# A transformer stack on one core: attention values weighted by features instead of by tokens, with a new order of the steps

## Chip, core and metric

The kernel runs on one NeuronCore of one Trainium2 chip. The metric is the device time of one execution in microseconds, the median of several runs; less is better. All data are float32.

## The reference

The input is 8 sequences of 512 tokens with 128 features. First comes one attention layer with squared-kernel features (stage one, not touched by the change but for one detail). Then six layers follow, each with a local attention and a feed-forward part. Cut to what matters:

```python
for i in range(6):
    t = shift_tokens(x)                      # second half of the features one token later
    q, k, v = heads(t @ Wqkv[i])             # 16 heads of 64
    q, k = l2norm(q) * qs, l2norm(k) * ks
    q, k = rotary(q), rotary(k)              # with a scale by position
    # windows of 32 tokens; each sees its own window and the one before: 64 keys
    sim = einsum('bhwie,bhwje->bhwij', q_w, k_2w) * 8
    attn = softmax(where(mask, -big, sim), -1)
    out = einsum('bhwij,bhwje->bhwie', attn, v_2w)
    x = out @ Wo[i] + x
    h = layernorm(shift_tokens(x)) * g + b
    a, gate = split(h @ W1[i] + b1)
    x = (a * gelu(gate)) @ W2[i] + b2 + x
```

A residual and layer norms stand around both stages.

## The kernel before, in words

The residual stream of each sequence lies in SBUF with features on partitions (`state`, L54). Work of the six layers is cut into **units** of 128 tokens: 6 layers x 8 sequences x 4 blocks = 192 units, made at L681 to L685. Four successive units are one sequence; below they are called a batch.

The loop over t (L703 to L739) is a software pipeline written out by hand. Turn t, a **slot**, runs steps of several units: `at(t, lag, step)` (L688) runs `step` for unit t-lag; with `ends=True` only for the last unit of a sequence. TensorE's order is exactly the order of these calls (manual schedule, L694). The orders of the other engines are made by a scheduler that places each instruction by its own estimate, with `tc.high_priority()` moving some ahead, and `issue_behind(later, earlier)` (L86) fixing an order of two instructions on one engine. Every engine then runs its instructions in that fixed order.

The steps of a slot, in TensorE's order:

- `proj(t, 0)` and `proj(t, 1)` (L409): q and k, two 128x512 products each into the PSUM ring `mm` (two buffers of two banks, L419). VectorE multiplies by the rotary tables (`turned` twice L429, `straight` L436), ScalarE squares (L444), GpSimd adds (L454). `sum_squares` (L456) sums the squares on VectorE; the one for k is put behind the last division by `issue_behind` (L461).
- `out_project(t-3)` (L598): eight products with the output weights, added into `state` by VectorE (L608).
- `by_keys(t-2)` (L556): eight transposes of the exponentials `pe`, copied out by ScalarE into `pT` (L564).
- `values(t)` (L474): v, two products, one ScalarE copy of both halves (L482) and eight DMAs that spread v to windows (L489, L490, L492).
- `by_features(t-1, 0)` and `(t-1, 4)` (L498): eight transposes each of q and k, copied by ScalarE (L514).
- `weigh_values(t-2)` (L566): 64 small products, with the weights (`pT`, 64 keys x 32 tokens) loaded and v (64 keys x 64 features) streamed. The result `po` has tokens on partitions. VectorE divides by the row sums as it copies out (`on`, L582).
- `feed_norm`, `feed_first`, `feed_middle`, `feed_last` (L611, L637, L648, L653), once in four slots each: norm over features after transposing `state` (its four transposes L616 go to ring `mm`), back to features, hidden products with Gelu, last product.
- `unit_length(t)` (L463): inverse root of the sums on ScalarE (`inverse_root`, L93), a minimum and two products on GpSimd (L467, L470).
- `scores(t-1)` (L519): the mask is put in by two products with the identity (L527), then 64 small products (L534). VectorE takes the maxima (`mx`, L542), ScalarE 16 exponentials (L546), VectorE the row sums `su` and their reciprocals (L552, L553).
- `out_by_features(t-2)` (L588): eight transposes of `on`, copied by ScalarE into `oT` (L596), which `out_project` of the next slot needs.

`sp` and `po` share one PSUM buffer of two banks (tag `s`, L525, L569), all transposes and `py` share a ring of two banks (tag `tr`). ScalarE needs two tables, one with logarithm and exponential (L76) and one with Gelu (L82); each batch loads both once.

## Time and profile before

| what | us |
|---|---|
| median of 3 runs (lowest, highest) | 3898.34 (3889.66, 3900.85) |
| the profiled execution itself | 3893.85 |
| its span by the profile | 3892.1 |
| TensorE busy, of 3892.1 | 3729.8 |
| VectorE / ScalarE / GpSimd busy | 2818.2 / 2657.5 / 1837.0 |
| L582, division, 192 times | 235.1 |
| L596, copies of `oT`, 384 times | 207.3 |
| L574, weighted values, 24576 records | 299.3 |
| L534, scores, 24576 records | 312.2 |
| transposes of `on`, 1536 records | 216.5 |
| L527, mask products, 384 records | 114.6 |

The granted TensorE clock is 0.99 of full speed. In the lines of groups, a row gives source line, engine, operation, the tile written and those read, the shapes, the count; then busy time, mean ns of one, and idle time of the engine before them with what ended it. In the chain and the timeline a row starts with the start and the duration in us. A float32 product is two records on TensorE, a transpose one; a small share of the records can be missing. The means of single matmuls contain their latency (225 ns for L574), so their cost is read from the chain's pieces, not from the means.

### The profile page before, as it was taken

What the parts mean: (1) busy time and instruction counts of PE and PEld (TensorE: products, weight loads), DVE (VectorE), ACT (ScalarE), POOL (GpSimd) and SP (SyncE); (2) the same over time, 40 slices, a digit from 0 to 9 for tenths busy, and PEclk for the clock granted to TensorE, in tenths of its full rate; (3) what the DMA queues carried; (4) which work ended last, traced back from release to release, by engine and by line L of the source; (5) the groups of instructions that cost most, each with busy time, mean ns of one, the idle gap of its engine ahead of it and who ended that gap; (6) DMA issues with size and microseconds to landing.
All of it is one profiled execution on the core that took longest, in us unless ns stands there. A gap on an engine that the chain in (4) does not pass through costs nothing.

```text
span 3892.1 us, 149565 instructions
## 1 busy us (share of the span) xinstructions
PE 3729.8 (96%) x65600; PEld 2474.2 (64%) x65600; DVE 2818.2 (72%) x4300; ACT 2657.5 (68%) x6745; POOL 1837.0 (47%) x1311
## 2 busy tenths in 40 slices
PE   8999989999999999999999999999999999999997
PEld 4555456666666666666666666666666666666665
DVE  4555567777867777777777777777787777777775
ACT  5565656776767777777777677777677777766664
POOL 0000025555555555555555555555555555555552
PEclk9999999999999999999999999999999999999998
DMA  2000012222222222222222322223222222222221
GB/s 81 17 9 12 6 50 71 59 66 60 76 74 63 63 63 66 71 75 65 60 62 64 82 65 66 65 56 82 70 66 59 66 65 56 65 68 68 64 67 37
DMA packets 153208, 233.46 MB, mean 60 GB/s; under 512 B 32622, under 2 KB 53356, under 8 KB 151788
## 3 DMA queue, kind: packets, MB, share of 16 engines
q1 hardware_dynamic: 152556, 223.89, 22.4%
q8 instruction: 517, 8.47, 0.9%
q14 instruction: 135, 1.11, 0.1%
HBM read 24.54 MB, written 4.19 MB: 7 GB/s over the span
## 4 chain that ended last, share of the span: by engine, by line
PE 89%; ACT 5%; issue 3%; DVE 2%; DMA 0%; POOL 0%; POOLq 0%; DVEq 0%; SPq 0%; ACTq 0%
PE tr L70 17%; PE mm L421 17%; PE mm L481 9%; PE py L603 9%; PE sp L534 7%; PE po L574 6%; PE y L282 4%; PE mm L625 3%; PE py L657 3%; PE mm L626 3%; PE sc L252 2%; PE sp L527 2%; ACT sq L444 2%; PE vv L230 2%; PE po L318 2%
## 5 line engine op out<-in xcount | busy, mean ns | idle before, releaser
L454 POOL TENSOR_TENSOR qk<-t,t 128x1024 f32<-128x1024 f32 x384 | 909.2, 2368 | 999.6 <-DVE t L436 999.5
L421 PE MATMUL mm<-wqkv,state 128*128 128x512 f32 x1536 | 727.1, 596 | 3.7 <-ACT v L482 2.6
L470 POOL TENSOR_TENSOR qk<-qk,ss 128x1024 f32<-128x1024 f32 x384 | 722.3, 1902 | 16.0
L429 DVE TENSOR_TENSOR t<-mm,tab 128x512 f32<-128x512 f32 x768 | 497.8, 685 | 242.8 <-PE mm L421 231.3
L546 ACT ACTIVATE pe<-sp,mx 128x64 f32<-128x64 f32 x3072 | 651.4, 376 | 27.6 <-DVE mx L542 27.3
L436 DVE TENSOR_TENSOR t<-mm,tab 128x1024 f32<-128x1024 f32 x384 | 465.9, 1213 | 0.0
L457 DVE TENSOR_REDUCE ss<-sq 128x16 f32<-128x1024 f32 x384 | 461.9, 1203 | 2.0 <-ACT sq L444 2.0
L444 ACT ACTIVATE sq<-mm 128x512 f32<-128x512 f32 x768 | 422.6, 610 | 47.2 <-DVE t L436 45.6
L603 PEld LDWEIGHTS py<-oT,wo 128*128 128x128 f32 x3072 | 374.8, 193 | 93.5 <-issue 56.2
L70 PEld LDWEIGHTS tr<-ident,qk 128*128 128x128 f32 x3072 | 345.7, 141 | 127.1 <-issue 105.7
L70 PE MATMUL tr<-ident,qk 128*128 128x128 f32 x3072 | 412.1, 277 | 7.4 <-ACT qT L514 2.3
L596 ACT COPY oT<-tr 128x512 f32<-128x512 f32 x384 | 207.3, 589 | 266.2 <-PE tr L70 265.2
L421 PEld LDWEIGHTS mm<-wqkv,state 128*128 128x128 f32 x1536 | 264.1, 192 | 191.6 <-issue 188.0
L481 PE MATMUL mm<-wqkv,state 128*128 128x512 f32 x768 | 367.9, 602 | 16.8 <-ACT sq L444 16.8
L603 PE MATMUL py<-oT,wo 128*128 128x128 f32 x3072 | 376.0, 276 | 1.0 <-ACT oT L596 0.9
L582 DVE TENSOR_TENSOR on<-po,su 128x1024 f32<-128x1024 f32 x192 | 235.1, 1224 | 170.1 <-PE po L574 170.1
L534 PEld LDWEIGHTS sp<-kT,qT 64*32 64x32 f32 x24576 | 271.9, 106 | 116.7 <-issue 113.8
L574 PE MATMUL po<-v,pT 64*32 64x64 f32 x24576 | 299.3, 225 | 44.7 <-issue 44.7
L482 ACT COPY v<-mm 128x1024 f32<-128x1024 f32 x192 | 194.5, 1013 | 211.0 <-PE mm L481 211.0
L534 PE MATMUL sp<-kT,qT 64*32 64x64 f32 x24576 | 312.2, 227 | 26.0 <-issue 25.2
L574 PEld LDWEIGHTS po<-v,pT 64*32 64x32 f32 x24576 | 258.5, 105 | 86.4 <-issue 86.2
L542 DVE TENSOR_REDUCE mx<-sp 128x16 f32<-128x1024 f32 x192 | 234.6, 1222 | 106.9 <-PE sp L534 106.3
(108 smaller groups left out, 5171.0 us busy)
## 6 DMA issues: line engine op xcount, KB each, us to landing
v<-v SPq DMA_DIRECT2D x1152, 128.0 KB
v<-v SPq DMA_DIRECT2D x672, 64.0 KB
wqkv<-in_L_ffn_Wqkv_dram SPq DMA_DIRECT2D x6, 1536.0 KB
wo<-in_L_ffn_Wo_dram SPq DMA_DIRECT2D x6, 512.0 KB
xin<-_attn_hidden_states_dram SPq DMA_DIRECT2D x8, 256.0 KB
xr<-_attn_hidden_states_dram SPq DMA_DIRECT2D x8, 256.0 KB
x<-xr SPq DMA_DIRECT2D x8, 256.0 KB
xr<-x SPq DMA_DIRECT2D x8, 256.0 KB
```

The lines of the kernel that those rows point to most:

```text
L70: nc.tensor.transpose(ps[:cols, :rows], src, ident[:rows, :rows])
L421: nc.tensor.matmul(ps[:, a].rearrange("p h d -> p (h d)"), lhs, wqkv[:, s, a, :], start=True, stop=True)
L429: nc.vector.tensor_tensor(t2[:, a], ps[:, 1 - a], tab[:, 2 * s + 1, j, HF * a : HF * (a + 1)].unsqueeze(1).to_broadcast([P, H, HF]), ALU.mult,
L436: nc.vector.tensor_tensor(t1, ps, tab[:, 2 * s, j, :].rearrange("p (a d) -> p a d", a=2).unsqueeze(2) .to_broadcast([P, 2, H, HF]), ALU.mult,)
L444: nc.scalar.activation(sq[:, :, a, :], ps[:, a], AF.Square)
L454: nc.gpsimd.tensor_tensor(qk[:, s].rearrange("p h a d -> p a h d"), t1, t2, ALU.add)
L470: nc.gpsimd.tensor_tensor(t, t, ss[:, i, :].unsqueeze(2).to_broadcast([P, H, HD]), ALU.mult)
L481: nc.tensor.matmul(ps[:, p, :], lhs, L["wqkv"][:, 2, p, :], start=True, stop=True)
L534: nc.tensor.matmul(sp[W * w : W * (w + 1), p, pair, :], qT[HD * p : HD * (p + 1), pair, W * w : W * (w + 1)], kT[HD * p : HD * (p + 1), pa ...
L546: ex = nc.scalar.activation(pe[:, pair, p, :], sp[:, p, pair, :], AF.Exp, bias=mx[:, p, pair : pair + 1])
L574: nc.tensor.matmul(po[W * w : W * (w + 1), p, pair, :], pT[r, pair, W * w : W * (w + 1)], v2[r, w, HD * pair : HD * (pair + 1)], start=Tru ...
L603: nc.tensor.matmul(py, L["wo"][:, c, :], oT[:, c, :], start=(c == 0), stop=(c == NP - 1))
```

## The change

1. `weigh_values` swaps its operands: v (64 keys x 64 features) is loaded and `pT` (64 keys x 32 tokens) is streamed, so `po` comes out with features on partitions. `on`, its division and `out_by_features` go; VectorE copies one half of `po` into `oT`, ScalarE the other. The rows of Wo are put in the matching order ahead of the launch.
2. The division moves before the transposes of `pe`: a new step `shares` (lag 2, ahead of `proj(t, 1)`) takes sums and reciprocals for each half of the heads on VectorE and divides `pe` in place on GpSimd.
3. `sp`, `po` and stage one's `y` become two tiles of one bank each (tags `s0`, `s1`), with maxima, exponentials and sums by half.
4. The mask products contract over 32 rows with a new constant `each`, apart from each sequence's first block.
5. `values` is cut into halves around `by_keys`; its copy and DMAs become `spread`, later in the slot. `by_features` is called for q and k apart, `squared` and `add_turned` become steps of their own.
6. `feed_norm` is split: `feed_in` transposes and copies (ScalarE) at lag 3, `feed_norm` follows at lag 4, `feed_first` moves to lag 5.
7. New `issue_behind` orders; the one that put the sum of k's squares behind the division goes. The Gelu table's load follows the copies of `pT`.
8. Once a batch, `addr_align(128, offset=46)` pads TensorE's instruction stream so that the next instruction stands 46 places after a multiple of 128.

```diff
     def gelu_only():
         ld = nc.scalar.preload_act_table_set("gelu_and_others")
-        issue_behind(ld, exps[-1])
+        issue_behind(ld, pcopies[-1])
...
+    def squared(u, s):
+        sq, ps = u["sq", s], u.pop(("psum", s))
+        for a in range(2):
+            q2 = nc.scalar.activation(sq[:, :, a, :], ps[:, a], AF.Square)
+            if s == 0 and exps:
+                issue_behind(q2, exps[-1])
+            if s == 1 and "cp" in u:
+                issue_behind(q2, u["cp"])
         if s == 0:
-            sum_squares(u, 0)
-        nc.gpsimd.tensor_tensor(qk[:, s].rearrange("p h a d -> p a h d"), t1, t2, ALU.add)
+            qsquares.append(q2)
+
+    def add_turned(u, s):
+        t1, t2 = u.pop("parts")
+        add = nc.gpsimd.tensor_tensor(u["qk"][:, s].rearrange("p h a d -> p a h d"), t1, t2, ALU.add)
+        if divisions:
+            issue_behind(add, divisions[-1])
...
-        if s == 1 and divisions:
-            issue_behind(su, divisions[-1])
+        if s == 0:
+            issue_behind(su, u["straight"])
...
+        nc.tensor.matmul(ps[:, half, :], lhs, L["wqkv"][:, 2, half, :], start=True, stop=True)
+
+    def spread(u):
+
+        j, v0 = u["j"], u["v0"]
+        cp = nc.scalar.copy(v0, u.pop("v0ps"))
+        if "cp" in u:
+            issue_behind(cp, u["cp"])
...
-        mk = mask0 if u["j"] == 0 else mask
-        sp = psum.tile([P, 2, NP, 2 * W], F32, tag="s", name="sp", bufs=1)
+        sp = [psum.tile([P, NP, 2 * W], F32, tag=f"s{p}", name="sp", bufs=1) for p in range(2)]
         for p in range(2):
+            r = slice(W * p, W * (p + 1))
+            lhs, mk = (identb, mask0) if u["j"] == 0 else (each[r], mask[r])
...
+    def shares(u):
+
+        pe = u["pe"]
+        for p in range(2):
+            part = pe[:, :, p]
+            su = f2.tile([P, NP], F32, tag=f"su{p}", name="su")
+            red = nc.vector.tensor_reduce(su, part, AX.X, ALU.add)
+            if sums:
+                issue_behind(red, sums[-1])
+            rc = nc.vector.reciprocal(su, su)
+            sums.append(rc)
+            with tc.high_priority():
+                dv = nc.gpsimd.tensor_tensor(
+                    part, part, su.unsqueeze(2).to_broadcast([P, NP, 2 * W]), ALU.mult
+                )
+        divisions.append(dv)
...
-        po = psum.tile([P, 2, NP, HD], F32, tag="s", name="po", bufs=1)
...
+        po = [psum.tile([P, NP // 2, P], F32, tag=f"s{p}", name="po", bufs=1) for p in range(2)]
+        for k in range(NP // 2):
             for w in range(4):
-                for p in range(2):
...
+                for i in range(2):
+                    for p in range(2):
+                        r, c, o = slice(HD * p, HD * (p + 1)), 2 * k + i, HD * (i ^ p)
+                        nc.tensor.matmul(
+                            po[p][o : o + HD, k, W * w : W * (w + 1)],
+                            v2[r, w, HD * c : HD * (c + 1)],
+                            pT[r, c, W * w : W * (w + 1)],
+                            start=True, stop=True, skip_group_check=True,
+                        )
+        u["oT"] = oT = f1.tile([P, 2, NP // 2, P], F32, tag="oT", name="oT")
         with tc.high_priority():
...
+            nc.vector.tensor_copy(oT[:, 0], po[0])
+            nc.scalar.copy(oT[:, 1], po[1])
...
         u["xn"] = xn = f1.tile([P, NB, DM], F32, tag="xn", name="xn")
-        layer_norm(f2, xn, ps, NB, by_log=True)
+        with tc.high_priority():
+            nc.scalar.copy(xn, ps)
+
+    def feed_norm(u):
+        layer_norm(f2, u["xn"], u["xn"], NB, by_log=True)
...
+            at(t, 0, proj, 0)
+            at(t, 3, out_project)
+            at(t, 0, squared, 0)
+            at(t, 2, shares)
+            at(t, 0, add_turned, 0)
+            at(t, 0, proj, 1)
+            at(t, 0, add_turned, 1)
+            at(t, 0, sum_squares, 0)
...
+            at(t, 1, by_features, 0, 0)
+            at(t, 1, by_features, 0, 1)
+            if t % NB == 0 and t <= len(units) - NB * (B - 1):
+                nc.tensor.addr_align(128, offset=IN_STEP)
+            at(t, 0, values, 0)
+            at(t, 2, by_keys)
+            at(t, 0, values, 1)
             if gelus:
                 gelu_only()
...
+            at(t, 5, feed_first, ends=True)
+            at(t, 1, by_features, 4, 0)
+            if 0 < t < len(units):
+                units[t]["cp"] = units[t - 1]["cp"]
+            at(t, 0, squared, 1)
             at(t, 2, weigh_values)
+            at(t, 4, feed_norm, ends=True)
             at(t, 0, sum_squares, 1)
             if not gelus:
                 at(t, 0, unit_length)
+            at(t, 1, by_features, 4, 1)
...
+            at(t, 3, feed_in, ends=True)
+            at(t, 0, spread)
             at(t, 5, feed_middle, ends=True)
...
             at(t, 6, feed_last, ends=True)
             at(t, 1, scores)
-            at(t, 2, out_by_features)
```

## The prediction

> **What bounds the kernel now.** I read the busy line and the chain first, then the chain in order of time over some slots, the timeline of the other engines, and the groups for durations. A slot is one turn of the loop over t (L703); four slots make a batch.

> ```profile
> PE 3729.8 (96%) x65600; PEld 2474.2 (64%) x65600; DVE 2818.2 (72%) x4300; ACT 2657.5 (68%) x6745; POOL 1837.0 (47%) x1311
> ...
> PE 89%; ACT 5%; issue 3%; DVE 2%; DMA 0%; POOL 0%; POOLq 0%; DVEq 0%; SPq 0%; ACTq 0%
> ```

> TensorE is the bound: 89% of the chain. One slot, from the end of the scores on:

> ```profile
> 1534.15 1.02 PE tr L70 x8
> 1535.17 1.72 PE mm L421 x4
> 1536.89 1.78 PE py L603 x16
> 1538.67 1.72 PE mm L421 x4
> 1540.39 0.87 PE tr L70 x8
> 1541.27 1.72 PE mm L481 x4
> 1542.98 0.88 PE tr L70 x8
> 1543.86 1.36 PE po L574 x88
> 1545.22 1.29 issue
> ```

> The reader is to see that PE goes from one step to the next without a gap: transposes of `on`, projection of q, output product, projection of k, transposes of `pe`, values, transposes of q and k, weighted values. The one hole is 1.29 us "issue" inside `po`. Scores start at 565.7 us and for the last time at about 3845.4 (timeline of L534), so 191 slots take 3280 us: 17.17 us a slot, **68.7 us a batch**.

> The other engines over the start of such a slot; the scores end, and the next step starts, at 1588.14:

> ```profile
> 1588.25 1.23 DVE L542 TENSOR_REDUCE mx<-sp 128x16 f32<-128x1024 f32 x1 [0.44 <-PE sp L534]
> ...
> 1591.06 1.29 DVE L429 TENSOR_TENSOR t<-mm,tab 128x512 f32<-128x512 f32 x2 [1.59 <-PE mm L421]
> 1592.27 1.21 DVE L436 TENSOR_TENSOR t<-mm,tab 128x1024 f32<-128x1024 f32 x1
> ...
> 1594.01 1.22 DVE L552 TENSOR_REDUCE su<-pe 128x16 f32<-128x1024 f32 x1
> ```

> The sum `su` is far down DVE's queue, 2.95 us after the first product with q's projection (1591.06), and nothing on PE waits for it soon: the transposes of `pe` need only the exponentials. Rows that price the change:

> ```profile
> L470 POOL TENSOR_TENSOR qk<-qk,ss 128x1024 f32<-128x1024 f32 x384 | 722.3, 1902 | 16.0
> ...
> L457 DVE TENSOR_REDUCE ss<-sq 128x16 f32<-128x1024 f32 x384 | 461.9, 1203 | 2.0 <-ACT sq L444 2.0
> ...
> L212 PE MATMUL vs<-cb,tw 128*128 128x4 f32 x128 | 15.6, 254 | 1.1 <-ACT tqk L222 1.0
> ```

> [...] L212 streams 4 columns and still takes 15.6/128 = 122 ns for 128 columns loaded [...] L574 and L534, 64x32 tiles, need 11 ns a record (1.41 us for 128); no row of before has a 64x64 tile. [...]

> **The change, part by part.**

> *Transposes of `on`* (8 a slot, 1.02 us of PE), the DVE product L582 (1.22) and two ACT copies L596 (0.54 each) go. In their place one DVE copy of half the size (0.69, as L234's 687 ns) and one ACT copy (0.59).

> *Weighted values by features.* 64 products as before, but 64 columns loaded and 32 streamed. [...] scaled by L212's 122 ns, 15. I take 128 x 14.6 = 1.87 us, an estimate, against 1.42. [...]

> *Masks.* In three slots of four they contract over 32 rows in two row groups; 0.43 becomes 0.22 to 0.43, I take 0.30.

> *Division moved to POOL, ahead of the transposes of `pe`.* Two products of 128x512 in the form of L470: half of 1.90, 0.95 to 1.05; I take 1.0. Bounds 0.5 and 1.3 (L327's 1266 ns for 512 plain columns). POOL has room (47%), but this puts DVE's sums and POOL on the path to PE. In the built order of the changed kernel DVE runs `mx` twice, the three products of q, two state additions, and then sum, reciprocal, sum, reciprocal. From the scores' end: products at 1.99 (PE's projection of q must end first; in the trace it began at 1589.07, after the 0.93 of the transposes that go, and the products at 1591.06), L436's at 3.20, state 4.33 (1593.40 in the same view, less the same 1589.07), first sum 4.94 to 5.63, reciprocal to 5.90, second sum 5.83 to 6.52, reciprocal to 6.79. POOL divides from 6.04 to 7.04 and to 8.04, and **the transposes of `pe` start at 8.2**. PE reaches them at 1.72+1.78+1.72+0.87+0.86 = 6.95: a new wait of 1.2 us a slot.

> *Order on ACT and DVE behind it.* Let b be that start. PE: transposes and second half of v to b+1.74, then four transposes of q. ACT copies them (b+2.38 to 2.97), and only then squares k (1.09, to b+4.03). DVE's sum of squares waits for this (b+4.13 to 5.34), and the copy out of `po` stands behind it on DVE (b+5.26 to 5.95), though `po` ended at b+4.06. The masks need that bank: b+6.0, where PE would be ready at b+4.5. Before, the copy out of `po` stood ahead of the sum. Scores end at b+6.0+0.3+1.45 = **b+7.75**. A plain slot is 8.2+7.75 = 15.95, whatever `po` takes up to 3.3 us.

> *Norm later.* By emission it moves a slot on; in the built order DVE still runs it in the slot of `feed_in`, wholly ahead of `mx`, and it now starts from an ACT copy. ACT: square to b+4.03, `oT`, k, `xn` copy to b+6.0; DVE: statistics 0.88 and 0.36 to b+7.25; ACT: v copy, then logarithm and exponential to b+7.96; DVE: four products to b+9.4. `mx` of the next slot starts 1.65 late, which is 0.9 at its products (2.9 for 1.99): b = 9.1 there.

> *Halves of v, spread.* Same 1.72 us of PE; v's copy is still in time for its bank and its DMAs keep more than a slot. Nothing on the path; if it slipped, projection of k would wait. *Alignment*: the batch is 2552 PE instructions, padded to 2560: 8 paddings at about 5.5 ns (256 in 1.41 us), nothing. The fetch holes (1.0 to 1.5 us, about two a batch) lie where PE now waits for the masks anyway: nothing left. *Five more table loads* at the stage edges: 5 x 1.28 = 6 us.

> Sum of a batch. Feed slot with the hidden products (5.2 us PE; the table load delays the square of k, and v's copy delays the second chunk): 20.65. Slot with the last product (2.58 hides the mask wait): 8.2+1.74+0.45+1.87+0.45+2.58+0.3+1.42 = 17.0. Slot with `feed_in`: 15.95. Slot after it: 9.1+7.75 = 16.85. **70.45 for 68.7**, so 191 slots cost 191 x (70.45-68.7)/4 = 84 us more, with the table loads 90: span 3982, execution 3984 (before: 3892.1 and 3893.85, which is 4.5 under the median shown, 3898.3). I predict **3980 us, slower by about 2%**. PE itself would need only some 62 us a batch: the change frees PE and is held by the ring mx, sums, division, transposes, square, sum, copy, masks, scores.

> **The rivals.**

> *Faster: the ring closes when PE arrives.* Place: POOL's division and the half sums. For it: every size there is scaled from whole tiles, and PE has 6 us a batch to gain. Against it: DVE's order is fixed and each link has a duration. If b is 7.0 where PE arrives, 191 x 1.2 = 230 us come off: 3750. It decides at b = 7.75 (0.45 less in each of four slots is the 1.75 of the sum): below it the kernel is faster. With a division of 0.5 us b is about 7.6: 3870.

> *Loads of 64 columns side by side fail*: `po` 3.7 us. It shows in full in the two feed slots (1.8 each) and by 0.35 in the others: 4.3 a batch, 205 us, 4185. For it: no 64x64 row; against it: the 64x32 tiles overlap more than two deep already.

> *Not what it says / nothing moves*: the gains and the new waits cancel, 3894. The sum's margin is 1.75 of 70, a few tenths a slot.

> **How the numbers follow.** Forecast 0.53 (3915 to 4060), faster rival 0.29, cancel 0.08, dear loads 0.10. A measurement of this kernel tells about 0.3% from no change. The range 3800 to 4070 leaves out the deeper half of the faster case (0.12) and the dear loads (0.08). With its own bounds alone the forecast would read 3915 to 4060. Faster 0.29, same 0.08, slower 0.63.

> **What would show it.** In the changed profile: PE's transposes of `pe` wait for POOL `pe` some 1.2 us in each slot, about 200 to 250 us in all; PE's masks wait for DVE `oT` in half the slots, 1.0 to 1.5 us each, 100 to 130 us; PE's share falls from 96% to near 90%; `po` takes 1.9 us; division 1.0 us. I am wrong if PE's share of the chain stays near 89%, if the transposes of `pe` don't wait, or if `po` takes over 3 us.

## The result and the profile after

The changed kernel takes 4211.0 us (median, 4197.8 to 4217.2) against 3894.0 us of the kernel before: ratio 1.081, interval 1.078 to 1.085. The forecast was 3980 (3800 to 4070): slower, but by 8.1% and not 2%. The profiled execution has a span of 4215.1 us.

The busy line and the chain of the page, which answer to 96% and 89% before:

```profile
PE 3773.3 (90%) x64064; PEld 2448.6 (58%) x64064; DVE 2916.8 (69%) x4884; ACT 2601.2 (62%) x6606; POOL 2220.7 (53%) x1695
...
PE 62%; DVE 16%; ACT 11%; POOL 7%; issue 3%; DMA 0%; POOLq 0%; DVEq 0%; ACTq 0%; SPq 0%
```

TensorE no longer sets the time: 27% of the chain has gone to VectorE, ScalarE and GpSimd. (Its busy time rose from 3729.8 us although it has fewer instructions; why is told further down.) One slot of the chain, from a division of one slot to the maxima of the next:

```profile
1996.03 1.05 POOL pe L598
1997.08 0.04 issue
1997.13 1.09 PE tr L78 x8
1998.22 0.86 PE mm L503 x2
1999.08 0.45 PE tr L78 x4
1999.53 0.02 issue
1999.56 0.58 ACT qT L542
2000.14 1.00 ACT sq L463 x2
2001.14 0.02 issue
2001.16 1.22 DVE ss L478
2002.38 0.61 DVE oT L631
2002.99 0.04 issue
2003.03 0.39 PE sp L559 x2
2003.42 1.41 PE sp L566 x91
2004.84 1.91 PE mm L429 x4
2006.75 1.80 PE py L639 x16
2008.55 0.04 issue
2008.59 0.59 DVE xn L123 x2
2009.18 0.61 DVE mx L575
```

This is the ring of the prediction, link by link: division, transposes of `pe`, copy of q, square of k, its sum, copy of `po`, masks, scores. What is not in the prediction stands at the end: the scores end at 2004.8, but `mx`, which needs nothing else, starts at 2009.1. VectorE and GpSimd there (timeline; start, duration, engine):

```profile
2004.04 0.36 DVE L115 BATCH_NORM_AGGREGATE ln_mv<-ln_st 128x2 f32<-128x6 f32 x4
...
2004.83 3.76 POOL L491 TENSOR_TENSOR qk<-qk,ss 128x1024 f32<-128x1024 f32 x2
2005.00 4.18 DVE L123 TENSOR_SCALAR xn<-xn,ln_mv,ln_rs 128x128 f32<-128x128 f32 x4 [0.60 <-ACT ln_rs L105]
2009.10 1.27 DVE L575 TENSOR_REDUCE mx<-sp 128x8 f32<-128x512 f32 x2
```

The norm's four products take 4.18 us, and GpSimd's two products beside them run through 3.76 us of it. These four alone (shortest, median and longest in ns):

```profile
L123 DVE TENSOR_SCALAR xn<-xn,ln_mv,ln_rs x4: 333/1072/1939, 2005.0 to 2008.8; 128x128 f32<-128x128 f32 x4
```

Two of the four are fast (0.33), two take 1.8 and 1.94. The groups over the run, and what TensorE waited for (us in all, times, longest):

```profile
L623 PE MATMUL po<-pT,v 64*64 64x32 f32 x24576 | 405.7, 222 | 0.0
L598 POOL TENSOR_TENSOR pe<-pe,su 128x512 f32<-128x512 f32 x384 | 392.4, 1042 | 683.7 <-DVE su L595 396.8 <-ACT sq L463 286.9
...
L123 DVE TENSOR_SCALAR xn<-xn,ln_mv,ln_rs 128x128 f32<-128x128 f32 x192 | 197.2, 1086 | 30.8 <-ACT ln_rs L105 30.8
```

```profile
PE tr L78 <- POOL pe L598: 166.7, 173, 4.5
PE tr L78 <- DVE state L644: 125.5, 47, 3.0
PE sp L559 <- DVE oT L631: 64.1, 98, 1.1
```

The first and third were forecast, but larger than found (200 to 250 and 100 to 130 us). The second was not: once a batch TensorE stands 2.7 us for the additions to `state`, which queue on VectorE behind that late `mx`.

Slots by kind, from one first score to the next (mean over all 48 batches, worked out from the trace):

| slot | forecast | after |
|---|---|---|
| with `feed_in` | 15.95 | 16.1 |
| after the norm | 16.85 | **20.3** |
| with the hidden products | 20.65 | 21.0 |
| with the last product | 17.0 | 18.0 |
| batch | 70.45 | 75.3 |

### The profile page after: what moved, and what is told of

It is laid out like the page before. It is cut to its first block, busy times and chain, and to the rows that moved or that the text cites. A ratio compares the mean times of both kernels' runs of the same rounds, so it can differ in the third digit from the quotient of the medians.

```text
span 4215.1 us, 147856 instructions
## 1 busy us (share of the span) xinstructions
PE 3773.3 (90%) x64064; PEld 2448.6 (58%) x64064; DVE 2916.8 (69%) x4884; ACT 2601.2 (62%) x6606; POOL 2220.7 (53%) x1695
## 4 chain that ended last, share of the span: by engine, by line
PE 62%; DVE 16%; ACT 11%; POOL 7%; issue 3%; DMA 0%; POOLq 0%; DVEq 0%; ACTq 0%; SPq 0%
PE tr L78 11%; PE mm L429 10%; POOL pe L598 7%; PE sp L566 7%; PE po L623 5%; PE mm L503 4%; ACT pe L579 4%; PE py L639 4%; PE y L290 4%; ACT sq L463 3%; DVE t L437 3%; PE mm L665 3%; PE py L697 3%; PE mm L666 3%; DVE ss L478 3%
## 5 line engine op out<-in xcount | busy, mean ns | idle before, releaser
L598 POOL TENSOR_TENSOR pe<-pe,su 128x512 f32<-128x512 f32 x384 | 392.4, 1042 | 683.7 <-DVE su L595 396.8
L429 PE MATMUL mm<-wqkv,state 128*128 128x512 f32 x1536 | 746.9, 609 | 1.1 <-ACT v L508 1.1
L491 POOL TENSOR_TENSOR qk<-qk,ss 128x1024 f32<-128x1024 f32 x384 | 722.2, 1902 | 16.0
L78 PE MATMUL tr<-ident,qk 128*128 128x128 f32 x3072 | 461.6, 282 | 129.0 <-DVE state L644 125.5
L503 PE MATMUL mm<-wqkv,state 128*128 128x512 f32 x768 | 442.0, 660 | 20.9 <-ACT sq L463 11.7
L611 ACT COPY pT<-tr 128x512 f32<-128x512 f32 x384 | 209.9, 589 | 389.5 <-PE tr L78 389.0
L623 PE MATMUL po<-pT,v 64*64 64x32 f32 x24576 | 405.7, 222 | 0.0
L623 PEld LDWEIGHTS po<-pT,v 64*64 64x64 f32 x24576 | 384.3, 137 | 35.5 <-issue 35.0
L78 PEld LDWEIGHTS tr<-ident,pe 128*128 128x128 f32 x1536 | 192.1, 158 | 346.5 <-POOL pe L598 345.4
L78 PE MATMUL tr<-ident,pe 128*128 128x128 f32 x1536 | 241.2, 307 | 167.6 <-POOL pe L598 166.7
L429 PEld LDWEIGHTS mm<-wqkv,state 128*128 128x128 f32 x1536 | 263.0, 191 | 205.4 <-issue 185.8
L575 DVE TENSOR_REDUCE mx<-sp 128x8 f32<-128x512 f32 x384 | 246.7, 683 | 157.5 <-PE sp L566 157.5
L542 ACT COPY qT<-tr 128x512 f32<-128x512 f32 x384 | 232.2, 605 | 166.3 <-PE tr L78 165.8
```

Source lines behind the costliest of these rows:

```text
L78: nc.tensor.transpose(ps[:cols, :rows], src, ident[:rows, :rows])
L429: nc.tensor.matmul(ps[:, a].rearrange("p h d -> p (h d)"), lhs, wqkv[:, s, a, :], start=True, stop=True)
L491: nc.gpsimd.tensor_tensor(t, t, ss[:, i, :].unsqueeze(2).to_broadcast([P, H, HD]), ALU.mult)
L503: nc.tensor.matmul(ps[:, half, :], lhs, L["wqkv"][:, 2, half, :], start=True, stop=True)
L598: dv = nc.gpsimd.tensor_tensor(part, part, su.unsqueeze(2).to_broadcast([P, NP, 2 * W]), ALU.mult)
L623: nc.tensor.matmul(po[p][o : o + HD, k, W * w : W * (w + 1)], v2[r, w, HD * c : HD * (c + 1)], pT[r, c, W * w : W * (w + 1)], start=True, ...
```

## Experiments

Edits are to the changed kernel unless said otherwise; ratios are to the kernel before.

**What makes the norm slow.** Three edits of the same four products.

```diff
 norm_from_psum:   products read nx (PSUM); statistics still from the copy
-                dst[:, j, :], src[:, j, :], mv[:, j, 0:1], ...
+                dst[:, j, :], prod[:, j, :], mv[:, j, 0:1], ...
...
-        layer_norm(f2, u["xn"], u["xn"], NB, by_log=True)
+        layer_norm(f2, u["xn"], u["xn"], NB, by_log=True, prod=u.pop("nx"))
 norm_other_tile:  products write another SBUF tile
-        layer_norm(f2, u["xn"], u["xn"], NB, by_log=True)
+        src = u["xn"]
+        u["xn"] = f1.tile([P, NB, DM], F32, tag="xn2", name="xn2")
+        layer_norm(f2, u["xn"], src, NB, by_log=True)
 norm_as_before:   feed_in and feed_norm together again, without the copy
-            nc.scalar.copy(xn, ps)
+        layer_norm(f2, xn, ps, NB, by_log=True)
```

> As the changed kernel, but the four products of the norm read the transposed state from PSUM (nx) and write xn to SBUF; the statistics still read ScalarE's copy. The changed kernel's products (xn from xn, both in SBUF) took 1086 ns in the mean while GpSimd ran its two products of qk, and before 402 ns from PSUM. Theory 1 (VectorE and GpSimd hold each other up when a VectorE product has SBUF on both sides): products back to about 0.40 us, the slot after feed_in from 20.3 to about 17, 48 x 3.2 = 140 to 160 us less, 4050 to 4075 us. Rival (what holds this slot is ScalarE's copy ahead of the norm or the order behind it): products may be shorter, but the time stays within 30 us of 4211.

Measured 4034.8 us, ratio to before 1.037 (1.035 to 1.039); slot after the norm 16.5.

> As the changed kernel, but the four products of the norm write a second SBUF tile in place of the one they read. Theory 1 (SBUF shared with GpSimd): products still 1.0 to 1.1 us, time unchanged, 4211 within 15 us. Rival (in place is what is slow: reading and writing one tile): products near 0.34 us, 4050 to 4075 us.

Measured 4205.0 us, 1.081 (1.080 to 1.083); slot 20.0.

> As the changed kernel, but the norm as before: no feed_in copy, statistics and products straight from PSUM in the same step at lag 3; feed_first stays at lag 5. Theory 1: products 0.40 us, the copy (0.6 us of ScalarE) gone too: the slot after feed_in about 16.5, 150 to 175 us less, 4035 to 4060 us. Rival (the later norm hides something else, the loss is in the operand swap and the division alone): within 40 us of 4211.

Measured 4017.0 us, 1.033 (1.032 to 1.035); slot 16.15.

And GpSimd taken away, with the norm left as it is:

```diff
 products_left_out
-        for i in range(2):
+        for i in range(2 if u["j"] != 2 else 0):
```

> The changed kernel, norm in place in SBUF as there, but GpSimd's two products that bring q and k to unit length are left out for the unit in each sequence (the third) whose products run beside the norm; so q and k of that unit stay unscaled. Theory (a product of VectorE with SBUF on both sides stands behind a whole GpSimd instruction): the trace of the changed kernel shows 95 of 320 of these products at 1.8 to 1.94 us, all of them under a GpSimd instruction, the other 225 at 0.34 to 0.41; with GpSimd quiet there all take 0.34, the slot after feed_in falls from 20.3 to about 16.8, 4040 to 4065 us. Rival (SBUF is slow for VectorE in that place for another reason, DMA say): products stay at 1.0 in the mean, 4190 to 4211 us.

Measured 4024.5 us, 1.034 (1.033 to 1.036); slot 16.2. The rows of the four kernels, one fence each in the order told (the second tile is called xn in its row too):

```profile
L123 DVE TENSOR_SCALAR xn<-nx,ln_mv,ln_rs 128x128 f32<-128x128 f32 x192 | 69.5, 404 | 30.8 <-ACT ln_rs L105 30.8
```

```profile
L123 DVE TENSOR_SCALAR xn<-xn,ln_mv,ln_rs 128x128 f32<-128x128 f32 x192 | 197.9, 1089 | 30.4 <-ACT ln_rs L105 30.4
```

```profile
L123 DVE TENSOR_SCALAR xn<-nx,ln_mv,ln_rs 128x128 f32<-128x128 f32 x192 | 65.6, 404 | 32.2 <-ACT ln_rs L105 28.8 <-DMA out_dram<-fo 3.5
```

```profile
L123 DVE TENSOR_SCALAR xn<-xn,ln_mv,ln_rs 128x128 f32<-128x128 f32 x192 | 53.6, 343 | 30.8 <-ACT ln_rs L105 30.8
```

404 ns from PSUM, 1089 from SBUF into whichever tile, 343 from SBUF when GpSimd is quiet. So it is neither the place in the queue nor the writing in place: for this product it is SBUF on both sides together with GpSimd. In the changed kernel's trace 94 of the norm's 192 products run while GpSimd runs and take 1.75 to 1.94 us (the expectation counted 95); the other 98 run while GpSimd is idle and take 0.33 to 0.35. So the fast two of the four shown did not escape: they came when GpSimd had ended. A slow product is about as long as one GpSimd product (median 1.875, and 3.76 / 2 = 1.88). From PSUM the same product runs wholly beside GpSimd in 188 of 192 cases in the trace of the kernel before, and takes 0.40 to 0.41 there. Not every operation is slowed: VectorE's copies of `po` from PSUM take 0.68 us under GpSimd and without it, and `bn_stats`, which reads and writes SBUF, took 0.28 in the five cases wholly under GpSimd. What tells the product from it, no run shows.

`mx` comes 2.6 us later than forecast (4.25 for 1.65), but the slot is 3.4 longer. Where the rest comes from, the granted clock by stretch tells (us; busy time and count of PE, PEld, DVE, ACT, POOL; PEclk; DMA share; GB/s):

```profile
2010.10:2013.10 3.00, 0.59 (x5) 0.35 (x3) 2.99 (x6) 3.00 (x17) 0.00 (x0) 1.00 0.43 107
2013.10:2016.40 3.30, 2.96 (x6) 1.02 (x6) 3.17 (x8) 2.09 (x5) 2.09 (x3) 0.57 0.00 0
2016.40:2019.10 2.70, 2.70 (x22) 2.00 (x23) 2.13 (x2) 1.08 (x3) 2.70 (x2) 0.89 0.00 0
```

TensorE is busy for 0.59 of 3.00 us while it waits for `state`, and then runs at 0.57 of its clock: in the slots after the norm the transposes of `pe` take 1.50 us in the mean for 0.94 in the others, the half of v behind them 1.18 for 0.87. In the clock record of this trace a stretch of half speed, 3.4 or 6.8 us long, comes with 42 of the 47 waits for `state`, which are 2.7 us each but the first (3.0). In the 3.4 us ahead of these drops TensorE had still been busy for 0.6 to 1.6 us. With the other five waits, as long, no drop came: what it takes, the runs do not show. The clock records of before and after hold only full and half speed. Over the run the mean granted clock is 0.967, so (1 - 0.967) x 2 x 4215 = 278 us at half clock; with the norm as before, counted alike, 0.990 of 4014.5, 80 us. Half of these 198 us is close to what TensorE's busy time rose by (3773.3 for 3680.0 us with the norm as before). It would also explain why the three edits that cured the norm came out 15 to 20 us below the ranges expected, which had the delay and not the clock. No run takes the halved clock away alone; its share is read from the traces.

**What the rest of the ring costs.** First one link alone:

```diff
 copy_before_sum
+        if s == 1 and ocopies:
+            issue_behind(su, ocopies[-1])
```

> As the changed kernel, but VectorE's sum of k's squares is put behind the copy out of po into oT, as it stood behind the division before. Theory (the copy queued behind the sum holds the masks up): the masks' wait for oT (63 us in the trace, up to 1.5 us in half the slots) goes, 60 to 105 us less, 4105 to 4150 us. Rival (the sum is now 0.7 us later, and inverse root, GpSimd's products and the transposes of q with it: the wait only moves): 4190 to 4211 us, with a new wait of PE for GpSimd's qk.

Measured 4223.7 us, 1.087 (1.085 to 1.088). The wait of the masks went, as the theory said (64.1 before):

```profile
PE tr L78 <- DVE state L646: 158.6, 47, 3.6
...
PE sp L561 <- DVE oT L633: 10.7, 51, 0.2
```

but the sum now stands between the copy and the norm, and the wait for `state` grew from 125.5 to 158.6, the clock fell to 0.962. The slot with `feed_in` gained 0.45, the two after it lost 0.1 and 0.3. Neither range holds the time: no gain, as the rival said, but 13 us above its upper end, and the wait is not at the place it named (transposes of q).

The next ones stand on norm_as_before (4017 us), to have the norm out of the way.

```diff
 undivided_keys
-                    part, part, su.unsqueeze(2)...
+                    off[:, :, p], part, su.unsqueeze(2)...
 late_keys
             at(t, 0, values, 0)
-            at(t, 2, by_keys)
             at(t, 0, values, 1)
...
             at(t, 1, by_features, 4, 0)
+            at(t, 2, by_keys)
```

> On the version with the norm as before (4017 us). GpSimd's division writes a scratch tile and the transposes of pe read the undivided exponentials: all instructions stay, only the way from sums and division to TensorE is cut; the output is not normalised. Theory (sums on VectorE and the division hold the transposes of pe up, some 1.8 us a slot in the trace of that version): the wait for GpSimd's pe goes, and VectorE's own row of work is next late (its copy of po after both sums of squares): 1.2 to 1.8 us a slot less, 3680 to 3790 us. Rival (the wait only moves, since VectorE's order ends the slot anyway): less than 0.5 us a slot, 3920 to 4017 us.

Measured 3780.8 us, 0.972 (0.970 to 0.975): the way through sums and division costs 236 us of norm_as_before. The slot with `feed_in` went from 16.0 to 14.8, the one after it from 16.15 to 14.9.

> On the version with the norm as before (4017 us). On TensorE the second half of v and the first transposes of q move ahead of the transposes of pe, so that TensorE has 1.3 us of work while the division runs. Theory (the division is merely too early asked for): wait for GpSimd's pe falls from 1.8 us to 0.4 to 0.6 a slot; behind it the square of k, the sum and the copy of po still hold the masks: 0.6 to 1.1 us a slot less, 3805 to 3900 us. Rival (the chain of square, sum and copy takes all back): 3980 to 4020 us.

Measured 3888.3 us, 0.9995 (0.998 to 1.001). TensorE's wait for GpSimd, 194.1 us in norm_as_before, is gone:

```profile
PE tr L78 <- ACT qT L542: 46.0, 188, 0.8
PE sp L559 <- DVE oT L631: 28.7, 53, 0.6
...
PE tr L78 <- POOL pe L598: 8.9, 2, 4.5
```

The time lies in the theory's range. So this wait, the largest that the forecast named, was only a matter of when the transposes are asked for, but 129 us came off and not 194. Between here and undivided_keys lie 107 us. About as much, 0.55 us in each of 192 slots, passes in late_keys between the transposes of `pe` and `po`, where TensorE now waits for ScalarE's copies. That the one is the other isn't shown: other waits differ too (the masks' is 28.7 here, 70.9 in undivided_keys).

> As late_keys (norm as before, transposes of pe later), and VectorE's copy of po ahead of the sum of k's squares. Theory (two links of one ring: alone, the copy's place gave nothing, since the later sum fed the late norm): 1.2 to 1.6 us a slot less than 4017, 3710 to 3790 us, below the kernel before. Rival (the sum that now ends later holds GpSimd's products and the transposes of q): 3850 to 3950 us, with a wait of TensorE for GpSimd's qk.

Measured 3890.2 us, 1.001 (1.000 to 1.002). This is the rival's range. The masks' wait went (28.7 to 9.4 us), and the slot with the hidden products took it back (20.4 to 20.7).

**The alignment.**

```diff
 no_alignment, late_keys_no_alignment
-                nc.tensor.addr_align(128, offset=IN_STEP)
```

> The changed kernel without the alignment of TensorE's instructions. Theory (holes of instruction fetch lie where TensorE waits anyway): within 15 us of 4211. Rival 1 (the alignment keeps one or two holes of 1.0 to 1.5 us a batch out of the dense stretches): 50 to 140 us slower. Rival 2 (the padding itself costs a hole): 50 to 70 us faster.

Measured 4210.8 us, 1.083 (1.080 to 1.086), the same as with it, as the theory said.

> As late_keys (norm as before, transposes of pe later; 3888 us), without the alignment of TensorE's instructions. There TensorE is busy 95% of the time, so a hole of instruction fetch is no longer hidden by a wait. Theory: now the places of the holes matter; without alignment the block ends wander through the batch (2552 is not a multiple of 256) and some hit the weighted values or scores: 10 to 50 us slower, 3900 to 3940 us. Rival (holes cost the same wherever they fall, or are hidden still): within 10 us of 3888.

Measured 3990.1 us, 1.027 (1.025 to 1.028): on a TensorE that hardly waits, the alignment is worth 102 us, twice what was expected. Then the offset alone, in late_keys:

```diff
 late_keys_offset_14 (78 and 110 alike)
-IN_STEP = 46
+IN_STEP = 14
```

> As late_keys (3888 us, offset 46) with offset 14: each block end falls 32 TensorE instructions elsewhere. Theory (what counts is where the ends fall in weighted values and scores): 3890 to 3990 us, different from 3888 by 30 us or more, in weighted values and scores only. Rival (only that they repeat counts): within 12 us of 3888.

> As late_keys with offset 78, 32 instructions to the other side. Theory: different from 3888 by 30 us or more, to either side, 3850 to 3990 us. Rival: within 12 us of 3888.

> As late_keys with offset 110, 64 instructions away, half the distance at which the alignment repeats. Theory: the farthest of the three, 3900 to 3990 us. Rival: within 12 us of 3888.

| late_keys with offset | us | "issue" before weighted values / scores | mean clock |
|---|---|---|---|
| 46 | 3888 | 3.7 / 12.3 | 0.989 |
| none | 3990 | 64.1 / 27.9 | 0.984 |
| 78 | 3993 | 8.8 / 53.6 | 0.988 |
| 14 | 4115 | 136.2 / 19.4 | 0.963 |
| 110 | 4140 | 158.7 / 29.2 | 0.965 |

The rows of the first and last, from the waits of TensorE:

```profile
PE sp L566 <- issue: 12.3, 9, 1.9
...
PE po L623 <- issue: 3.7, 2, 1.9
```

```profile
PE po L623 <- issue: 158.7, 93, 4.1
PE sp L566 <- issue: 29.2, 45, 1.9
```

That there are such blocks the traces show: an instruction queue (q8) brought 517 packets of 16 KiB in the kernel before for TensorE's 132355 records and 506 in the changed one for 129613, 256 a packet, and the 69 holes of over 0.7 us inside weighted values and scores of before all stand at the same place of 256 records. The place of the block ends counts, as the theory said, and 110 is the farthest; but 14 and 110 lie 125 and 150 us beyond its upper end, and 78 lies 3. Same instructions, same order, 64 places apart: 6.5%. The holes account for 172 us of the 252, and half of the added time at half clock ((1 - 0.965) x 2 x 4144.5 = 290 us, 86 in late_keys) for some 100 by estimate, together a little more than is measured. For offset 78 the clock stays, and the holes alone (57.5 more before transposes) make 104 of 105 us.

```diff
 before_aligned (to the kernel before)
+            if t % NB == 0 and t <= len(units) - NB * (B - 1):
+                nc.tensor.addr_align(128, offset=46)
             at(t, 0, values)
```

> The kernel before with the alignment alone, once in each batch, at the start of v's products (same call, same offset of 46). Its holes (weighted values and scores over their usual 1.41 us) come to about 2.3 us a batch in the trace. Theory (aligned block ends repeat in each batch, but its batch isn't a whole number of blocks and the offset was not chosen for its order; the padding costs some 0.4 us): within 40 us of 3889, no sure gain. Rival (the alignment as such takes the holes away): 60 to 100 us faster, 3790 to 3830 us.

Measured 4108.9 us, 1.056 (1.054 to 1.058): neither. Its batch needs much more padding (in the trace of before it is 2619 records, 69 short of a multiple of 128), and TensorE stands still ahead of v, where the padding is, 40 times for 4.1 us in the mean, then runs at 0.57 of its clock for 3.5 us in the place shown (waits of TensorE; then the chain, 1.72 us being the usual time of v):

```profile
PE mm L481 <- issue: 162.7, 40, 6.8
```

```profile
1556.58 2.83 issue
1559.41 3.46 PE mm L481 x4
```

**Orders that were to beat both.** All have the norm as before and the copy of `po` ahead of the sum. The steps in TensorE's order, the feed-forward left out:

```diff
 early_sums (the alignment is left out too)
+proj 0, shares, out_project, straight_q, proj 1, by_features (0, 0), (0, 1), by_keys,
+by_features (4, 0), weigh_values, values 0, 1, by_features (4, 1), scores
 early_sums_split
-            at(t, 2, shares)
+            at(t, 2, shares, 0)
             at(t, 3, out_project)
+            at(t, 2, shares, 1)
 output_product_between (to late_keys_copy_first, offset 14)
-            at(t, 3, out_project)
...
             at(t, 2, by_keys)
+            at(t, 3, out_project)
 k_before_values (to late_keys_copy_first, offset 38)
+            at(t, 1, by_features, 4, 1)
             at(t, 2, weigh_values)
...
-            at(t, 1, by_features, 4, 1)
```

> All that the runs point to in one order, every computation kept: norm as before; VectorE takes sums and reciprocals of the exponentials ahead of its third product of q, so that GpSimd divides 2 us earlier; transposes of pe go straight behind the first transposes of q and k; weighted values follow, and both halves of v come behind them to hide the copy of po, which goes ahead of the sum of k's squares; square of q behind the copies of pT. Theory (the ring division, copy of po, masks is what holds the slot, and it can be hidden): plain slot 14.1 to 14.6 us for 16.0, 3680 to 3760 us, under the kernel before. Rival (ScalarE's squares, now later, hold v's bank or the sum): waits of TensorE for sq of 1 us a slot, 3850 to 3950 us.

Measured 3971.3 us, 1.020 (1.018 to 1.022), above both. TensorE waited for `state` 68.9 us and for GpSimd 47.0. Though not aligned, it has hardly a hole (1.3 and 2.3 us of issue before weighted values and scores, 64.1 and 27.9 in late_keys_no_alignment). v's 1.8 us now stand between weighted values and scores; whether that is why was not tested.

> As early_sums, but the two additions to the residual stream stand between the two sums of VectorE, not behind both. In early_sums (3971 us) TensorE waited for them at the first transposes of k (the bank that the output product still held): 0.6 us in plain slots, 1.7 in the slot after feed_in. Theory: this goes, the second division is 0.6 us later and costs 0.4 again: 1.5 to 2.5 us a batch less, 3850 to 3900 us. Rival (the division, 0.6 us later, takes all of it back): 3950 to 3980 us.

Measured 3984.8 us, 1.025 (1.024 to 1.027), about where the rival had it: the first wait went, the second became 158.9.

> As late_keys_copy_first (norm as before, transposes of pe later, copy of po ahead of the sum of k's squares), and the output product moves from the start of the slot to between the transposes of pe and the weighted values; offset 14 in place of 46, since 32 instructions now stand between (the block ends then fall in weighted values and scores as in late_keys). Theory: the output product hides the copies of pT (0.55 us a slot), VectorE's sums no longer stand behind the additions of the output product (0.6 us), so the transposes of pe don't wait either: 0.5 to 0.9 us a slot less than 3888, 3720 to 3800 us, below the kernel before. Rival (TensorE's instructions as such bound it, the waits being taken up already): 3860 to 3900 us.

Measured 4182.7 us, 1.076 (1.075 to 1.078), outside both. TensorE now asks for v's bank before ScalarE has squared q: 147.2 us of wait there, and 72.6 for the norm's bank in the slot after it.

> As late_keys_copy_first (3890 us), with the second four transposes of k moved ahead of the weighted values, the squares of k behind the copies of pT and the copy of v behind that of po on ScalarE; offset 38 in place of 46, since eight more instructions stand ahead of the weighted values. Theory: the transposes cover the wait for pT (0.44 of 0.55 us a slot), and the masks pay 0.3 us of it back in half the slots: 1.0 to 1.5 us a batch less, 3815 to 3845 us, below the kernel before. Rival (the masks now wait for the copy of po in full, 0.5 us more in each slot): 3880 to 3930 us.

Measured 3973.6 us, 1.022 (1.021 to 1.023), outside both. The transposes of k share two banks with those of `pe`, so they wait for the same copy of `pT`: the 0.46 before the weighted values stayed, and the masks' wait came on top (50.3 us). The largest new wait is a third: in the slot after the norm v's products stand 1.3 us for ScalarE's squares (60.0 us in all, 1.1 in late_keys_copy_first). The edit also changed ScalarE's order, and no run separates that from the moved transposes.

No order that keeps the whole computation is faster than the kernel before; late_keys is level with it.

## Why the prediction was right in direction and wrong in size

- *The ring, and its start.* Right. b, the start of the transposes of `pe` from the scores' end, was forecast at 8.2: in the slot with `feed_in` it is 1.82 + 1.78 + 1.72 + 0.90 + 2.03 = 8.25, the last term holding a wait of 1.17 (forecast 1.2). The division took 1.04 us (1.0). undivided_keys shows that this link is a cause, not only a companion. The sum took every engine to run in the order built: in the traces of both kernels all instructions of VectorE, ScalarE and GpSimd that name a tile stand in it (4884, 6504 and 1695 here).
- *The norm.* **This is the step that failed.** "DVE: four products to b+9.4" priced them at 1.44 us (from b+7.96), about what four took that read PSUM in the kernel before (two in 0.73 us). That GpSimd runs beside them was put at nothing, without a reason. The change turned their operand from PSUM to SBUF, and the same four took 4.18 in the slot shown. `mx` came 4.3 us late and not 1.65, b there was 11.6 and not 9.1. TensorE's clock fell to 0.57 in the stretch shown after the wait that follows, which no term of the sum had; the rest of the slot took 8.7 for 7.75. Together 3.4 us in each of 48 batches, 165 us of the 231 that are missing. norm_as_before takes 194 us away, of which the forecast had some 43 (0.9 x 48).
- *The slot with the last product.* 18.0 for 17.0, 46 us. In the last layer the final norm's transposes stand behind that product, which the sum left out: these slots take 20.0, the others 17.7, 0.3 in the mean. The rest is in the whole masks of the next sequence's first block (0.53, where 0.30 was put in), scores 1.57 for 1.42, weighted values 2.00 for 1.87.
- *Weighted values.* 2.00 us a slot against 1.87. The price, 15 ns a record scaled from L212's 122 ns and taken as 14.6, was the author's estimate of how loads of 64 columns overlap, which no row of before shows; it is 15.6. The loads overlap: a record of L623's takes 137 ns in the mean, one of L574's before took 105 at 11 ns a record. The rival of 3.7 us is out.
- *The masks' wait.* Forecast 1.5, found 0.65 in the slot with `feed_in`: TensorE was later (its transposes of `nx`, 0.44, were left out of the comparison), so the start of the masks was right. What it would bring to remove it was never in the sum; copy_before_sum shows: nothing, while the norm stands behind the sum.
- *Alignment.* "Nothing" is right for this kernel (4211 with and without), and the reason given, that TensorE waits anyway, fits: without alignment its holes come to 29.5 us here and to 105 in late_keys_no_alignment. In late_keys, where it hardly does, it was wrong by 102 us.
- *"PE itself would need only some 62 us a batch."* Not shown. The shortest batch of any run is 66.4, in undivided_keys with TensorE 96% busy, which makes 63.9 of work; late_keys has 68.5 at 95%.

The direction rests on a ring that the runs confirm; that the time fell outside the range is the norm's doing, which none of the rivals named: with the norm cured by any of the three edits it is 4017 to 4035 us, inside the range. The faster rival needed b below 7.75; it is 8.25. Where the transposes were asked for later, 129 us came back, which with the norm as before made the kernel level with the one before and not faster. Whether an order exists that hides all of them stays open.

## What to carry to other kernels

Price an elementwise step by where its operands lie and by who runs beside it: the same product cost 0.34, 0.40 or 1.9 us. When a buffer moves from PSUM to SBUF, look up what GpSimd does at that time. When the first engine begins to wait, ask whether its gaps come near the 2.7 us that came with half speed here; and when it stops waiting, look at where its instruction blocks end, which cost nothing in this kernel while it waited and 102 us in late_keys.
